# Edges counted in 162 groups of 256 with bands of 12 places, instead of 110 groups of 375 with bands of 16

## The chip, the cores and the metric

The kernel runs on one core of a Trainium2 chip. The metric is the device time of one execution in microseconds, median of the runs. Engines are called as in the profile: PE is TensorE's matmuls and PEld its weight loads, DVE is VectorE, ACT ScalarE, POOL GpSimd, SP SyncE. A row of the profile names a line of the kernel (L521), an engine, an operation and the tiles written and read.

## The reference

Two layers of a graph network over 1250 nodes with 1024 features and 41,250 edges, sorted by destination. The first layer is a relational convolution with two edge types, the second an attention over edges.

```python
h = relu(layernorm(x))
# layer 0: t5 norm, then for r in (0, 1):
    w = (edge_type == r)
    sums = segment_sum(h[src] @ W_rel[r] * w, dst); cnt = segment_sum(w, dst)
    out = x @ W_root + bias + sums / max(cnt, 1)
x = x + h + elu(out) @ wo
# layer 1: h = relu(layernorm(x)) @ W; e = exp(-leaky_relu(al[src] + ar[dst]))
x = x + elu(segment_sum(e * h[dst], src) / (segment_sum(e, src) + 1e-5))
```

## The kernel before

The kernel does not gather rows. It counts how many edges of each type lead from each node to each other node, in a table `cnt` (source within a tile of 128, tile of the source and type, destination), and turns the segment sums into matmuls with that table. The change is in the counting, in `fast_arm`.

**Counting.** The edges, in order of destination, are cut into NG groups of J chunks of PE_ edges, one edge to a partition. For a chunk, DVE builds `key` (L520): for each edge a row of 2 T W columns (T = 10 tiles of sources, two types, W places of destinations), with a one where the column number equals the edge's key. For two groups at a time it builds `lo` (L495, `low_hots`): a one-hot row of 128 for the source within its tile. PE multiplies the two (L521) into the accumulator `acc` of the group, so that `acc` holds the counts for W consecutive destinations, beginning at the first destination of the group. A node whose edges reach over a group's end is finished by a carry: a matmul of 2 T columns (L524) that adds the last chunk's edges of that node to the next group's accumulator. Its one-hot rows `hot_ck` are made by `carry_hots` in four portions. ACT loads the group's first destination into a register (`values_load`, L526) and writes the accumulator into `cnt` at that column (the eviction, L528). Evictions overlap by columns, so each waits for the one before.

**What stands around it.** In the same stage, PE multiplies the normalized rows of ten tiles `t` with the weights of layer 0: 16 products for a tile (L721, `mm<-w,hT`, 429 columns, two passes each). After product `i` of tile `t` as many chunks are emitted as keep the two in step:

```python
want = min(NG * J, -(-NG * J * max(t * SK + i + 1 - late, 0) // (T * SK - 6 - late)))
some(want - done)
```

`plan` puts the other work of the stage at fixed products: the statistics of a later tile (L543), its normalized rows `h` (`norm`, L558), its square sums and their root (`square`, L564 and L566), the two times four transposes of the next tile (`turn`, L576, at products 8 and 10), the copies that scale them into `hT` (`scaled`, L583, at 9 and 12), and the three parts of the previous tile's result `y` (L597 to L614, at 3, 7 and 10). The order written in these loops is the order on PE, DVE and ACT (a manual schedule).

**Banks.** Accumulators with `q % 4 == 3` have a PSUM bank of their own; the others take turns in three banks that they share with the transposes:

```python
def bank(name, dtype=F32):
    return ps.tile([128, 4, 128], dtype, name=name, tag="tp", bufs=3)
...
acc = (own_bank if q % 4 == 3 else bank)("acc").rearrange("p a b -> p (a b)")
```

A bank is free again when ACT has evicted or copied what is in it. `key` has five buffers, `lo` two.

**Afterwards.** The means over neighbours (L798) read `cnt` and `y` tile by tile, then follow the rest of layer 0 and layer 1. If a group's destinations reach over its band, `count_over` sees it, and a general arm computes everything again.

Of the kernel before, what the change touches and what calls it, by code (L numbers as in the profile page):

```python
# [8 lines left out]
F32 = mybir.dt.float32  # L9
# [17 lines left out]
N = 1250  # L27
T = 10
ROWS = [min(128, N - t * 128) for t in range(T)]
PE_ = 125  # L30
J = 3
GE = J * PE_
NG = 110
W = 16
NPAD = 1280


# [373 lines left out]
def fast_arm(tc, ctx, edges, firsts, w_root, conv_bias, wo, w_gat, a_gat, out,  # L411
# [6 lines left out]
    F = w_root.shape[1]  # L418
# [53 lines left out]
    with ExitStack() as c1:  # L472
# [28 lines left out]
        def carry_hots(q, q1):  # L501
            nc.vector.tensor_tensor(hot_ck[:, q:q1], iota_ck[:, None, :].to_broadcast([PE_, q1 - q, 2 * T]),
                                    ck[:, q:q1, None].to_broadcast([PE_, q1 - q, 2 * T]), ALU.is_equal)

        def chunks():

            for q in range(NG):
                if q % 2 == 0 and q // 2 not in los:
                    low_hots(q)
                if q in (10, 40, 75):  # L510
                    carry_hots(q, {10: 40, 40: 75, 75: NG}[q])
                acc = (own_bank if q % 4 == 3 else bank)("acc").rearrange("p a b -> p (a b)")
                a3 = acc[:, :2 * T * W].rearrange("p (c w) -> p c w", w=W)
                if q:

                    last = los[(q - 1) // 2][:, :, ((q - 1) % 2) * J + J - 1]
                    carry = (a3[:, :, 0:1], last, hot_ck[:, q - 1, :, None])
                for j in range(J):
                    key = hot.tile([PE_, 2 * T * W], BF16, name="key")
                    nc.vector.tensor_scalar(key, iota_key, keys[:, q, j:j + 1], None, op0=ALU.is_equal)  # L520
                    nc.tensor.matmul(acc[:, :2 * T * W], los[q // 2][:, :, (q % 2) * J + j], key, start=(j == 0),  # L521
                                     stop=(j == J - 1))
                    if q and j == 0:
                        nc.tensor.matmul(*carry, start=False, stop=False)  # L524
                    if j == J - 1:
                        b = nc.values_load(first[0:1, q:q + 1], engines=[mybir.EngineType.Activation],  # L526
                                           min_val=0, max_val=N - 1)
                        nc.scalar.activation(cnt_w[:, :, bass.ds(b, W)], a3, AF.Copy)  # L528
                    yield
# [86 lines left out]

        tile_of = room[1][:PE_, :NG * J].bitcast(I32).rearrange("p (q j) -> p q j", j=J)
        block, d = (room[1][:PE_, i * NG * J:(i + 1) * NG * J].rearrange("p (q j) -> p q j", j=J) for i in (1, 2))
        step, firstf, limit, over = (room[2][:PE_, a * NG:b * NG] for a, b in ((1, 2), (2, 3), (3, 6), (6, 9)))
        limit, over = (v.rearrange("p (q j) -> p q j", j=J) for v in (limit, over))  # L620

        for i in range(2):
# [13 lines left out]
        def carried():  # L636


            nc.vector.tensor_tensor(step[:, :NG - 1], first[:, 1:], first[:, :NG - 1], ALU.subtract)
            nc.vector.tensor_scalar(step[:, NG - 1:], first[:, NG - 1:], -1.0, float(N), op0=ALU.mult, op1=ALU.add)  # L640

            for j in range(J):
                nc.gpsimd.tensor_scalar(limit[:, :, j], step, -1.0 if j < J - 1 else 0.0, W - 1.0,
                                        op0=ALU.add, op1=ALU.min)
            nc.gpsimd.tensor_copy(firstf, first)
            nc.vector.tensor_tensor(ck, d[:, :, J - 1], step, ALU.is_equal)
            nc.vector.scalar_tensor_tensor(ck, block[:, :, J - 1], 1.0, ck, op0=ALU.add, op1=ALU.mult)
            carry_hots(0, 10)

        worst = small("worst")  # L650

# [20 lines left out]
        def clear_if_odd():  # L672

            odd = nc.values_load(n_odd, engines=[mybir.EngineType.Activation], min_val=0, max_val=8192)
            with tc.If(odd > 0):
# [23 lines left out]
        late_plan = {(1, 1): lambda: square(1), (1, 2): lambda: norm(2), (1, 12): lambda: square(2),  # L699
                     (2, 1): lambda: count_over(), (2, 4): lambda: turn_worst(), (2, 6): lambda: worst_over(),  # L700
                     (2, 12): lambda: clear_if_odd()}
        done, late = 0, 5
        SK = 2 * KD
        for t in range(T):
            pys[t] = ps.tile([128, 2, 512], F32, name="mm")
            for i in range(SK):
# [18 lines left out]
                done = max(done, want)  # L725
# [689 lines left out]
@with_exitstack  # L1415
def gnn_kernel(
    ctx: ExitStack,
    tc: tile.TileContext,
    x: bass.AP,
    src: bass.AP,  # L1420
    dst: bass.AP,
    etype: bass.AP,
    ln_w: bass.AP,
    w_rel: bass.AP,
    w_root: bass.AP,
    conv_bias: bass.AP,
    wo: bass.AP,
    w_gat: bass.AP,
    a_gat: bass.AP,
    edges: bass.AP,  # L1430
    firsts: bass.AP,
    w_cat: bass.AP,
    lnw_cols: bass.AP,
    out: bass.AP,
):


    nc = tc.nc
    D = x.shape[1]
    F = w_root.shape[1]  # L1440
    KD = D // 128
    assert x.shape[0] == N and NG * GE == src.shape[0] and F % 2 == 0

    const = ctx.enter_context(tc.tile_pool(name="const", bufs=1))
    big = ctx.enter_context(tc.tile_pool(name="big", bufs=1))

    def large_tiles():
        return ([big.tile([128, D + 2], F32, name=f"x{t}", tag=f"x{t}")[:, :D] for t in range(T)],
                big.tile([128, 2 * T * NPAD], F16, name="cnt", tag="cnt"),
                [big.tile([128, D + 2], F32, name=f"w{k}", tag=f"w{k}") for k in range(KD)])  # L1450


    xs, cnt_raw, wt = large_tiles()
    wcat = [w[:, :3 * F].rearrange("p (r f) -> p r f", r=2) for w in wt]

    def load_x(t):
        nc.sync.dma_start(xs[t][:ROWS[t]], x[t * 128:t * 128 + ROWS[t], :])

    def loads(part):

        if part == 0:
            for c in (slice(0, 512), slice(512, D)):
                nc.sync.dma_start(xs[0][:, c], x[:128, c])
        for k in range(1) if part == 0 else range(1, KD):
            nc.sync.dma_start(wt[k][:, :3 * F], w_cat[k * 128:(k + 1) * 128, :])
            if k == 3:
                load_x(1)
        if part == 0:
            return
        nc.sync.dma_start(bias, _bcast_rows(conv_bias, 128, F))  # L1470
        for t in range(2, T):
            load_x(t)

    eps5 = const.tile([128, 1], F32, name="eps5")
    nc.vector.memset(eps5, 1e-5)
    eps6 = const.tile([128, 1], F32, name="eps6")
    nc.vector.memset(eps6, 1e-6)
    ones = const.tile([128, 1], F32, name="ones")
    lnw = const.tile([128, KD], F32, name="lnw")
    nc.scalar.dma_start(lnw, lnw_cols)  # L1480

    nc.scalar.activation(ones, eps5, AF.Sqrt)
    bias = const.tile([128, F], F32, name="bias")
    ident = const.tile([128, 128], F32, name="ident")
    make_identity(nc, ident)
    n_odd = const.tile([1, 1], I32, name="n_odd")

    meta = const.tile([128, 2376], F32, name="meta")
    parts, at = [], 0
    for size in (NG * J, NG * J // 2, NG * T, 3 * 128, T * W, T, NG, NG):  # L1490
        parts.append(meta[:PE_, at:at + size])
        at += size
    keys = parts[0].rearrange("p (q j) -> p q j", j=J)
    lows = parts[1].bitcast(F16).rearrange("p (q j) -> p q j", j=J)
    hot_ck = parts[2].bitcast(BF16).rearrange("p (q c) -> p q c", c=2 * T)
    iota_lo = parts[3].bitcast(F16).rearrange("p (l j) -> p l j", j=2 * J)
    nc.vector.memset(ones, 1.0)
    iota_key, iota_ck, ck = parts[4].bitcast(F16), parts[5].bitcast(F16), parts[6]
    firsts_at = meta[:, at - NG:at].bitcast(I32)
    nc.gpsimd.iota(iota_key, pattern=[[1, 2 * T * W]], base=0, channel_multiplier=0,  # L1500
                   allow_small_or_imprecise_dtypes=True)
    nc.gpsimd.iota(iota_lo, pattern=[[1, 128], [0, 2 * J]], base=0, channel_multiplier=0,
                   allow_small_or_imprecise_dtypes=True)
    nc.gpsimd.iota(iota_ck, pattern=[[1, 2 * T]], base=1, channel_multiplier=0,
                   allow_small_or_imprecise_dtypes=True)
    nc.gpsimd.memset(cnt_raw.rearrange("p (c n) -> p c n", n=NPAD)[:, :, N:], 0.0)

    with ExitStack() as arm:
        fast_arm(tc, arm, edges, firsts, w_root, conv_bias, wo, w_gat, a_gat, out, ident, eps5, eps6, lnw, const,
                 big, wt, wcat, bias, xs, cnt_raw, meta, keys, lows, hot_ck, ck, firsts_at, n_odd, iota_lo, iota_key, iota_ck,  # L1510
                 loads)

    odd = nc.values_load(n_odd, min_val=0, max_val=8192)
    with tc.If(odd > 0):
        with ExitStack() as arm:
            xs, cnt_raw, wt = large_tiles()
            general_arm(tc, arm, x, src, dst, etype, ln_w, w_rel, w_root, conv_bias, wo, w_gat, a_gat, out,
                        ident, ones, eps5, eps6, const, [w[:, :D] for w in wt], xs, cnt_raw)
# [6 lines left out]
def _laid_out(inputs):  # L1525

    import numpy as _np

    lists = _np.stack([inputs['src'], inputs['edge_type_2'], inputs['dst']])
    rel, root = inputs['L0_gnn_W_rel'], inputs['L0_gnn_W_root']  # L1530
    half = root.shape[1] // 2
    return {
# [32 lines left out]
```

## Time and profile before

| | |
|---|---|
| median of 3 runs | 592.57 us (592.41 to 592.61) |
| profiled execution | 591.38 us |
| span of the profile | 589.6 us |
| products L721 | x320 passes, 143.7 us busy |
| chunks L521 | x330, 72.3 us busy |
| carries L524 | x109, 19.8 us busy |
| keys L520 on DVE | x330, 85.2 us busy |
| low halves L495 on DVE | x55, 30.3 us busy |
| evictions L528 on ACT | x110, 49.9 us busy |

Busy times of overlapping instructions on PE are counted once, and the recorded duration of a matmul reaches to its last write, so what a matmul costs PE is read from the distance of starts, not from its duration.

### The profile page before, as it was taken

What the parts mean: (1) busy time and instruction counts of PE and PEld (TensorE: products, weight loads), DVE (VectorE), ACT (ScalarE), POOL (GpSimd) and SP (SyncE); (2) the same over time, 40 slices, a digit from 0 to 9 for tenths busy, and PEclk for the clock granted to TensorE, in tenths of its full rate; (3) what the DMA queues carried; (4) which work ended last, traced back from release to release, by engine and by line L of the source; (5) the groups of instructions that cost most, each with busy time, mean ns of one, the idle gap of its engine ahead of it and who ended that gap; (6) DMA issues with size and microseconds to landing.
All of it is one profiled execution on the core that took longest, in us unless ns stands there. A gap on an engine that the chain in (4) does not pass through costs nothing.

```text
span 589.6 us, 8473 instructions
## 1 busy us (share of the span) xinstructions
PE 577.0 (98%) x2848; PEld 419.4 (71%) x2848; DVE 417.9 (71%) x1031; ACT 274.3 (47%) x642; POOL 27.9 (5%) x42
## 2 busy tenths in 40 slices
PE   8999999999999999999999999999999999999994
PEld 5666666666665776776766788888888778888873
DVE  5889887898773666648899926141749988887732
ACT  4666566655643000002332124253727488887722
POOL 5010000000000000000000000000033000000000
PEclk9999999999999999999999999999999999999998
DMA  8950111101106910010015730000010122222221
GB/s 287 345 142 6 36 37 37 36 2 36 29 0 214 245 42 36 37 72 37 36 72 164 209 100 1 0 1 1 2 37 2 37 93 88 71 83 82 99 69 51
DMA packets 21931, 43.82 MB, mean 74 GB/s; under 512 B 2638, under 2 KB 7886, under 8 KB 21876
## 3 DMA queue, kind: packets, MB, share of 16 engines
q1 hardware_dynamic: 20308, 38.05, 19.2%
q0 software_dynamic: 1424, 5.12, 4.6%
q8 instruction: 24, 0.39, 0.3%
q14 instruction: 31, 0.25, 0.1%
q10 hardware_dynamic: 144, 0.00, 0.0%
HBM read 24.53 MB, written 13.52 MB: 65 GB/s over the span
## 4 chain that ended last, share of the span: by engine, by line
PE 80%; DVE 11%; issue 3%; DMA 3%; ACT 2%; SPq 0%; POOL 0%; ACTq 0%; DVEq 0%; POOLq 0%
PE mm L721 17%; PE mm L798 12%; PE mm L989 11%; PE tp L1159 11%; PE acc L521 7%; PE mm L1159 7%; PE mm L844 5%; PE z L989 5%; DMA w<-in_w_cat_dram 3%; DVE cnt L1051 2%; DVE hm L1138 2%; PE tp L576 1%; DVE cnt L1049 1%; ACT d L1097 1%; DVE zm L1134 1%
## 5 line engine op out<-in xcount | busy, mean ns | idle before, releaser
L721 PE MATMUL mm<-w,hT 128*128 128x429 f32 (+1 forms) x320 | 143.7, 535 | 0.9 <-DMA w<-in_w_cat_dram 0.9
L520 DVE TENSOR_SCALAR key<-meta 125x320 bf16<-125x320 f16 x330 | 85.2, 300 | 24.1 <-PE acc L521 12.0
L528 ACT ACTIVATE cnt<-acc 128x320 f32 x110 | 49.9, 453 | 69.5 <-PE acc L521 60.9
L521 PEld LDWEIGHTS <-lo 125*128 125x128 bf16 x330 | 40.5, 126 | 50.4 <-issue 37.0
L798 PE MATMUL mm<-y,cnt 128*128 128x286 bf16 (+3 forms) x600 | 75.2, 285 | 0.4 <-DVE y L614 0.4
L521 PE MATMUL acc<-key,lo 125*128 125x320 bf16 x330 | 72.3, 303 | 0.0
L798 PEld LDWEIGHTS <-cnt 128*128 128x128 f16 (+1 forms) x600 | 59.5, 99 | 14.7 <-issue 1.0
L721 PEld LDWEIGHTS mm<-w,hT 128*128 128x128 f32 (+1 forms) x320 | 51.4, 191 | 6.2 <-issue 3.3
L989 PE MATMUL mm<-w,a 128*128 128x257 f32 (+3 forms) x192 | 44.5, 379 | 0.0
L809 ACT ACTIVATE bias<-bias 128x286 f32<-128x286 f32 (+1 forms) x10 | 4.4, 442 | 80.2 <-DVE bias L808 80.2
L989 PEld LDWEIGHTS mm<-w,a 128*128 128x128 f32 (+1 forms) x192 | 35.7, 187 | 5.5 <-ACT h L1015 0.2
L844 PE MATMUL mm<-wo,meta 128*128 128x512 f32 (+1 forms) x80 | 37.6, 592 | 0.0
L1097 ACT ACTIVATE d<-meta,score 128x128 f32<-128x128 f32 x84 | 27.2, 389 | 10.7 <-DVE d L1114 10.7
L1159 PE MATMUL tp<-hm,zm 128*128 128x512 f32 (+1 forms) x120 | 30.1, 400 | 0.5 <-ACT tp L1165 0.5
L495 DVE TENSOR_TENSOR lo<-meta 125x768 bf16<-125x768 f16 x55 | 30.3, 551 | 0.1
L1097 ACT ACTIVATE d<-meta,tenths 128x128 f32<-128x128 f32 x84 | 27.2, 390 | 0.0
L1159 PEld LDWEIGHTS tp<-hm,zm 128*128 128x128 f32 (+1 forms) x120 | 21.6, 184 | 5.9 <-ACT tp L1165 0.6
L1159 PE MATMUL tp<-hh,zh 128*128 128x512 f32 (+3 forms) x60 | 23.8, 396 | 0.0
L1159 PE MATMUL tp<-parts,zl 128*128 128x512 f32 (+3 forms) x60 | 23.7, 395 | 0.0
L1159 PE MATMUL tp<-hh,parts 128*128 128x512 f32 (+1 forms) x60 | 23.7, 395 | 0.0
L1159 PE MATMUL tp<-parts 128*128 128x512 f32 (+1 forms) x60 | 23.6, 393 | 0.0
L844 PEld LDWEIGHTS mm<-wo,meta 128*128 128x128 f32 (+1 forms) x80 | 14.4, 187 | 12.9 <-issue 12.1
(207 smaller groups left out, 1007.1 us busy)
## 6 DMA issues: line engine op xcount, KB each, us to landing
x<-h POOLq DMA_DIRECT2D x9, 512.0 KB, 4.6
xd<-x SPq DMA_DIRECT2D x9, 512.0 KB, 2.6
x<-in_x_dram SPq DMA_DIRECT2D x8, 512.0 KB, 12.1
w<-in_L_gnn_W_dram SPq DMA_DIRECT2D x8, 512.0 KB, 7.1
w<-in_w_cat_dram SPq DMA_DIRECT2D x8, 429.0 KB, 9.9
squares<-cnt SPq DMA_DIRECT2D x10, 320.0 KB, 3.3
d<-squares SPq DMA_DIRECT2D x40, 80.0 KB, 2.2
d<-xd SPq DMA_DIRECT2D x9, 256.0 KB, 2.8
```

Source lines behind the costliest of these rows:

```text
L495: nc.vector.tensor_tensor(los[q // 2], iota_lo, lows[:, q:q + 2, :].rearrange("p q j -> p (q j)")[:, None, :].to_broadcast([PE_, 128, 2 * J]),
L520: nc.vector.tensor_scalar(key, iota_key, keys[:, q, j:j + 1], None, op0=ALU.is_equal)
L521: nc.tensor.matmul(acc[:, :2 * T * W], los[q // 2][:, :, (q % 2) * J + j], key, start=(j == 0), stop=(j == J - 1))
L528: nc.scalar.activation(cnt_w[:, :, bass.ds(b, W)], a3, AF.Copy)
L721: nc.tensor.matmul(pys[t][:ROWS[t], r, :F + HF], hTs[t][0][:, k, :ROWS[t]], wcat[k][:, r, :], start=(k == 0), stop=(k == KD - 1))
L798: nc.tensor.matmul(pm[:n, r, :f], cnt[:k, h, r, t * 128:t * 128 + n], ybs[h][:k, s, r, :f], start=(h == 0 and s == 0), stop=(h == T - 1 an ...
L844: nc.tensor.matmul(po[:n, c, :], oT[:, i, :n], wo_of[i][:, cs], start=(i == 0), stop=False)
L989: nc.tensor.matmul(o[:a.shape[2], :c1 - c0], a[:, k, :], b[k][:, c0:c1], start=(start and k == 0), stop=(k == KH - 1), skip_group_check=no ...
L1051: nc.vector.transpose(turned_tot.rearrange("p (c t j) -> p c t j", c=4, t=T), tot.rearrange("p (t c i) -> p c t i", t=T, c=4))
L1097: nc.scalar.activation(form[:, t - t0, :], rows[:, s, :], AF.Exp, bias=n[:, t:t + 1], scale=scale)
L1138: engine.tensor_tensor(hms[t][:n, :D], low(t)[:n].bitcast(F32), hhs[t][:n, :D].bitcast(F32), ALU.subtract)
L1159: nc.tensor.matmul(sums_of[s, c][:n], at(sets[s % 2][f], t, t + 1)[:k, 0, :n], h[:k, c * HD:c * HD + HD], start=(t == 0 and f == "h"), sto ...
```

## The change

The groups become smaller: two chunks of 128 edges instead of three of 125, 162 groups instead of 110, with a band of 12 destinations instead of 16. A chunk's matmul, key and eviction have 240 columns instead of 320, `lo` is made for two groups at a time as before (512 instead of 768 elements a row). The last group is padded on the host with edges that match no key. The portions of `carry_hots` and the start of the chunks (`late`, one product later) move along.

```diff
-PE_ = 125
-J = 3
+PE_ = 128
+J = 2
 GE = J * PE_
-NG = 110
-W = 16
+NG = 162
+W = 12
...
+        CARRIES = {15: 60, 60: 111, 111: NG}
...
-                if q in (10, 40, 75):
-                    carry_hots(q, {10: 40, 40: 75, 75: NG}[q])
+                if q in CARRIES:
+                    carry_hots(q, CARRIES[q])
...
-            carry_hots(0, 10)
+            carry_hots(0, 15)
...
-        done, late = 0, 5
+        done, late = 0, 6
...
-    meta = const.tile([128, 2376], F32, name="meta")
+    meta = const.tile([128, 2816], F32, name="meta")
...
-    lists = _np.stack([inputs['src'], inputs['edge_type_2'], inputs['dst']])
+    behind = (0, NG * GE - inputs['src'].shape[0])
+    lists = _np.stack([_np.pad(inputs['src'], behind, constant_values=32767), _np.pad(inputs['edge_type_2'], behind),
+                       _np.pad(inputs['dst'], behind, mode='edge')])
```

In the changed kernel the lines of the stage lie two further down: L523 is the chunk, L526 the carry, L528 the register, L530 the eviction, L578 the transposes, L585 the scaled copies, L723 the products.

More of the change, by code (lines that the diff above doesn't have):

```diff
@@ L618, in fast_arm @@
         block, d = (room[1][:PE_, i * NG * J:(i + 1) * NG * J].rearrange("p (q j) -> p q j", j=J) for i in (1, 2))
-        step, firstf, limit, over = (room[2][:PE_, a * NG:b * NG] for a, b in ((1, 2), (2, 3), (3, 6), (6, 9)))
+        step, firstf, limit, over = (room[2][:PE_, a * NG:b * NG] for a, b in ((1, 2), (2, 3), (3, 3 + J), (3 + J, 3 + 2 * J)))
         limit, over = (v.rearrange("p (q j) -> p q j", j=J) for v in (limit, over))
@@ L1441, in gnn_kernel @@
     KD = D // 128
-    assert x.shape[0] == N and NG * GE == src.shape[0] and F % 2 == 0
+    assert x.shape[0] == N and 0 <= NG * GE - src.shape[0] < GE and F % 2 == 0
     const = ctx.enter_context(tc.tile_pool(name="const", bufs=1))
@@ L1486, in gnn_kernel @@
     n_odd = const.tile([1, 1], I32, name="n_odd")
-    meta = const.tile([128, 2376], F32, name="meta")
+    meta = const.tile([128, 2816], F32, name="meta")
     parts, at = [], 0
-    for size in (NG * J, NG * J // 2, NG * T, 3 * 128, T * W, T, NG, NG):
+    for size in (NG * J, NG * J // 2, NG * T, J * 128, T * W, T, NG, NG):
         parts.append(meta[:PE_, at:at + size])
```

## The prediction

> **What bounds the kernel now.** I read the page first: span, busy shares, slices.
>
> ```profile
> span 589.6 us, 8473 instructions
> PE 577.0 (98%) x2848; PEld 419.4 (71%) x2848; DVE 417.9 (71%) x1031; ACT 274.3 (47%) x642; POOL 27.9 (5%) x42
> ...
> PEclk9999999999999999999999999999999999999998
> ```
>
> TensorE is the bound and runs at its full granted clock. The edges are counted in the first 182 us. The table by stretches gives that stage from 24.5 us, where the loads are in, to its last count:
>
> ```profile
> 24.50:181.70 157.20, 157.20 (x757) 97.70 (x756) 130.88 (x444) 95.56 (x232) 8.56 (x18) 1.00 0.20 44
> ```
>
> PE is never idle, DVE is busy for 130.9 of 157.2 us, ACT for 95.6 (61%). The timeline of PE alone gives prices, as differences of starts, since the durations overlap:
>
> ```profile
> 43.03 0.18 PE L524 MATMUL acc<-meta,lo 125*128 125x20 bf16 x1
> 43.06 0.97 PE L721 MATMUL mm<-w,hT 128*128 128x429 f32 x2
> 43.86 0.44 PE L521 MATMUL acc<-key,lo 125*128 125x320 bf16 x2
> 44.14 0.88 PE L721 MATMUL mm<-w,hT 128*128 128x429 f32 x2
> 44.86 0.30 PE L521 MATMUL acc<-key,lo 125*128 125x320 bf16 x1
> 45.00 0.18 PE L524 MATMUL acc<-meta,lo 125*128 125x20 bf16 x1
> 45.02 0.46 PE L521 MATMUL acc<-key,lo 125*128 125x320 bf16 x2
> ```
>
> A chunk of 320 columns holds PE for 0.14 us, a carry for 0.03, a product (two passes) for 0.72, but for 0.80 where a carry stands just ahead of it (43.06 to 43.86): the carry is too short to cover the load of the product's weights. Over the whole stretch the means are 140.6, 26.7, 722 and 803 ns.
>
> ACT looks idle, but its timeline and the rows of its queue say otherwise:
>
> ```profile
> 99.88 0.44 ACT L528 ACTIVATE cnt<-acc 128x320 f32 x1 [0.53 <-PE acc L524]
> 100.60 0.48 ACT L528 ACTIVATE cnt<-acc 128x320 f32 x1 [0.28 <-ACT cnt L528]
> 101.31 0.44 ACT L528 ACTIVATE cnt<-acc 128x320 f32 x1 [0.23 <-ACT cnt L528]
> ```
>
> ```profile
> L526 ACTq TENSOR_LOAD <-meta x110: 272/278/1110, 9.3 to 180.8; - x110
> L526 ACTq FUSED_REGOPS  x110: 147/147/166, 9.9 to 181.2; - x110
> ```
>
> Three evictions that had nothing to wait for follow each other by 0.715 us, though each lasts 0.44. Between them ACT's queue loads the group's first node into a register: 278 ns, then 147, 18 and 42 with the gaps between them. So an eviction costs 0.715 us whatever its width, and ACT's busy share hides it.
>
> The last view is the timeline of PE and ACT at a bank's reuse:
>
> ```profile
> 58.96 1.13 ACT L583 ACTIVATE hT<-tp,lnw 128x128 f32<-128x128 f32 x4
> ...
> 59.89 0.44 PE L521 MATMUL acc<-key,lo 125*128 125x320 bf16 x2
> ```
>
> Accumulators of groups with q%4 below 3 share three banks with the transposes. The second chunk of the lower row (60.03, group 30) takes the bank that ACT's copies of the upper row give back at 60.09: no slack at all (starts precede recorded ends by 0.06). I worked out this slack for every bank: about 0 at groups 18 and 30, 0.2 at 42, 0.3 to 0.5 us once in most other tiles. PE is the bound today, but ACT stands right behind it.
>
> **The change on PE.** Before 18.64 us PE waits for weights in any case (0.2 us idle there), so I count what follows: 318 chunks before, 315 after (the start one product later moves three chunks behind that wait). A chunk falls from 320 to 240 columns, a width that the trace lacks. The bf16 products of L798 move 286 columns in 122.7 ns (60 of them in 7.36 us), 0.43 a column, so 80 columns are worth at most 34.3; from the carry's 26.7 for 20 columns up to that row the slope is 0.36, so at least 28.9. I take 33, near the wide row: 107.6 a chunk. 318 x 0.1406 = 44.7; 315 x 0.1076 = 33.9: -10.8 us (-9.5 to -11.2). Carries after that point go from 106 to 157: +51 x 0.0267 = +1.4. By the order of instructions, a carry stands directly before a product 66 times instead of 42: +24 x 0.081 = +1.9. Four transposes in a row hold PE 109 ns each, which I read as the load of f32 weights; a chunk of 107.6 covers it but for 0 to 6 ns, at 73 places 0 to 0.4 us: I take 0.1. Sum on PE: -7.4 us, between -5.8 and -7.9.
>
> **The other engines.** DVE: a key costs 0.214 us start to start, 330 of them 70.6; 324 narrower ones lie between 52 (in proportion) and 69 (no fall). Low halves, 55 x 0.469 = 25.8, become 81 of two thirds the width, 25 to 38; carry hots +1.1. At its worst DVE rises by 12 to 143 us of some 155, likelier it falls; keys end 1.3 to 1.7 us ahead of their matmul in half of the cases: nothing on the path. POOL's narrower constants end before use: nothing. The first nodes grow by 28 KB in a load phase that moves some 320 GB/s: +0.1 us. Padding needs no chip time. The spread of the lists is safe: worked out from the reference's lists, no group of 256 reaches further than 10 places, so the general arm stays off.
>
> ACT gets 52 more evictions. Narrower ones (0.44 to about 0.36 us) don't help, since the register chain sets 0.715. Per tile of 18.15 us today: 11 x 0.715 = 7.9, plus what other work adds to the distance between two evictions, from the shortest distances in the trace: copy of y 0.46, of its rest 0.49, root and four scaled copies 0.80, four copies 0.60, normalized rows 0.75, square and root 2.0, together 5.1. Sum 13.0. After: 16.2 x 0.715 + 5.1 = 16.7 us, while PE's tile shrinks to 18.15 - 7.4/9 = 17.3. ACT would be loaded to 96%, with four banks to smooth bursts of up to 4 us (copies, square and root together: 3.8 to 4.0 in the trace).
>
> The Trainium skill, Perfetto Trace Analysis, "Optimizing Scalar/DVE Operations", gives about 51 ns of fixed access cost for a ScalarE instruction on PSUM and advises grouping into larger operations once the engine is saturated. By that price alone 52 more evictions are an estimated 2.7 us of ACT, and the sum would keep PE's gain; the 0.715 us of the trace makes them 37 us. The advice speaks against the change, its price understates it.
>
> **Where ACT holds PE up.** I follow one tile in the changed order (the fourth), with the durations above, from the start of the second four transposes as zero. PE: transposes 0.44, four products, seven chunks, three carries (0.44 + 2.89 + 0.75 + 0.08): it wants the transposes' bank back, for the third group on that ring, at 4.15. ACT: the first eviction can start when its last chunk, behind the next product, is done, 1.54; the next, 0.715 on, 2.26; normalized rows, then the third at 3.63; the four scaled copies behind it end at 4.99, and the bank is free 0.06 earlier, 4.93. PE stands for 0.78 us. Today the same stretch (55.41 to 60.03) takes PE 4.62 and ACT 4.68. The second transposes of that tile already waited for the bank of the first: only two groups now lie between them, 0.61. I did the same for all tiles, with the slow register loads that the trace has after each square (0.87, then 0.45 us, while the residual's DMA runs). Waits, by tile from the end of tile 0: 1.6, 2.0, 3.0, 0.9, 1.4, 0, 1.4, 1.7, 0, 0.1: 12.1 us. The same rules on the old order return most of the measured slacks within 0.05 us, and 0.5 us of waits that the trace lacks, so I take 11.6. With all register loads at 278 ns it would be 10.
>
> **Sum.** -7.4 + 11.6 + 0.1 = +4.3 us. The profiled execution is 591.38 (span 589.6 and 1.8 around it); the median of the runs is 592.57, 1.2 above. The rest of the span only shifts. The last eviction, due some 3.7 us before the stage's last product ends (182.5 against 186.1 today), stays hidden. Forecast 592.57 + 4.3 = 596.9 us; its own range, with waits of 9 to 14 and PE's bounds, 593.8 to 600.5.
>
> **Rivals.** A: *ACT keeps up and PE keeps its gain.* It needs banks back some 0.8 us earlier per tile than my count, for instance if the queue hides the register load behind a wait. For it: ACT's 61%. Against: 0.06 us of slack today and evictions 0.715 apart with nothing to wait for. It gives 592.57 - 7.3 = 585.3; the time is below today's as long as the waits stay under 7.3 us. Chance 0.10.
>
> B: *waits just cancel the gain*, 6.1 to 8.5 us of them: 591.4 to 593.8, within 0.2%, about what a measurement of this kernel can tell from no change. Chance 0.07.
>
> C: *ACT becomes the full bound*: other work doesn't overlap the register chain at all, or loads are slow far more often (0.6 to 1.0 us is common up to 26 us). A tile is then 11.6 + 6.6 (the ACT work in it by durations) = 18.2 plus the waits of PE for bursts, some 19: about +8 us, 600 to 603. Chance 0.08.
>
> The granted clock stays at 1.00 even from 7 to 13 us, where PE idles 0.8 us in all, so I add nothing for it. The Trainium skill, TensorE: Matmul & The Clock Gate, "A second HAM failure mode: psum-queue depth-cycling", tells of a clock that falls back when PE idles often between groups; no run here shows that.
>
> D: *the change does something else* (general arm runs): excluded above, under 0.01.
>
> Main case 0.75. The range of 592 to 600.5 leaves out A, a part of B and the end of C. Slower by over 0.2%: 0.83, faster 0.10.
>
> **What the profile after would show.** Right: L523 at some 225 to 270 ns x324, L530 x162 still 0.715 apart at its densest, PE idle 9 to 13 us before L523 and L578 with ACT (scaled copies L585, evictions L530) as releaser, first product of the last tile near 175 instead of 171 us, the stage from 190.2 on unchanged at 399 us. Wrong: no PE idle in the stage, or DVE's key as releaser; evictions less than 0.6 us apart; or a granted clock below 1.

## The result, and the profile after

The changed kernel takes 593.88 us (median of 12 runs, 592.93 to 594.58), the kernel before 592.48 in the same comparison (12 runs). The ratio is 1.0023, with a 95% interval of 1.0015 to 1.0031: slower by 1.4 us, where 4.3 were forecast. The profiled execution took 593.43 us, 2.05 above that of before: 1.0 us of it is in the counting stage, 0.1 between that and the last matmul, 0.9 behind the last matmul. Single executions differ by about as much as that last part, so the sum below goes by medians. Later comparisons put the kernel before at 592.2 to 592.4.

The head of the page after, and the counting stage in the table by stretches (columns: PE, PEld, DVE, ACT, POOL busy with counts, granted clock, DMA share, GB/s):

```profile
span 591.6 us, 8893 instructions
...
PE 571.1 (97%) x2894; PEld 412.1 (70%) x2894; DVE 412.0 (70%) x1051; ACT 284.2 (48%) x694; POOL 25.6 (4%) x41
...
L530 ACT ACTIVATE cnt<-acc 128x240 f32 x162 | 63.5, 392 | 61.0 <-PE acc L523 38.5
...
L523 PE MATMUL acc<-key,lo 128*128 128x240 bf16 x324 | 61.6, 268 | 4.7 <-ACT cnt L530 3.9
```

```profile
24.50:182.70 158.20, 151.89 (x804) 90.83 (x803) 126.39 (x466) 106.23 (x287) 8.18 (x18) 1.00 0.20 45
```

PE, which was busy for all of the stage, now idles for 6.3 us of it by its recorded durations. By the distances of starts, each beyond what the same instructions in the same order usually take, it waits some 8.6 us. The clock is unchanged. DVE is busy for 126.4 of 158.2 us, less than before. The page names the releaser at the chunks, ACT's eviction. One such wait, in the timeline of PE and ACT:

```profile
64.21 1.03 ACT L566 ACTIVATE sq<-h 128x1024 f32<-128x1024 f32 x1
...
65.12 0.27 PE L523 MATMUL acc<-key,lo 128*128 128x240 bf16 x1
65.15 0.19 ACT L566 ACTIVATION_READ_ACCUMULATOR sq<-h 128x1 f32 x1
...
65.37 0.29 ACT L568 ACTIVATE rms<-ssq,eps 128x1 f32<-128x1 f32 x1
66.03 0.44 ACT L530 ACTIVATE cnt<-acc 128x240 f32 x1 [0.37 <-issue]
66.52 0.27 PE L523 MATMUL acc<-key,lo 128*128 128x240 bf16 x1 [1.12 <-ACT cnt L530]
66.62 0.18 PE L526 MATMUL acc<-meta,lo 128*128 128x20 bf16 x1
66.65 0.61 PE L723 MATMUL mm<-w,hT 128*128 128x429 f32 x1
66.75 0.44 ACT L530 ACTIVATE cnt<-acc 128x240 f32 x1 [0.29 <-ACT cnt L530]
```

ACT squares a tile; its queue stands until the square is done, issues the root (65.37), loads the register, and evicts only at 66.03. PE's next group needs that bank and starts 1.40 us after the last chunk (65.12 to 66.52) instead of 0.1. The two evictions at the end are 0.72 us apart: the width of 240 columns changed the median duration of an eviction (377 ns, from 441) and not this spacing. The register rows are those of before:

```profile
L528 ACTq TENSOR_LOAD <-meta x162: 270/276/1188, 9.7 to 182.1; - x162
L528 ACTq FUSED_REGOPS  x162: 147/147/170, 10.2 to 182.4; - x162
```

### The profile page after: what moved, and what is told of

It reads as the page before. It is cut to its first block, busy times and chain, and to the rows that moved or that the text cites. A ratio compares the mean times of both kernels' runs of the same rounds, so it can differ in the third digit from the quotient of the medians.

```text
span 591.6 us, 8893 instructions
## 1 busy us (share of the span) xinstructions
PE 571.1 (97%) x2894; PEld 412.1 (70%) x2894; DVE 412.0 (70%) x1051; ACT 284.2 (48%) x694; POOL 25.6 (4%) x41
## 5 line engine op out<-in xcount | busy, mean ns | idle before, releaser
L723 PE MATMUL mm<-w,hT 128*128 128x429 f32 (+1 forms) x320 | 145.8, 542 | 1.7 <-DMA w<-in_w_cat_dram 1.7
L530 ACT ACTIVATE cnt<-acc 128x240 f32 x162 | 63.5, 392 | 61.0 <-PE acc L523 38.5
L522 DVE TENSOR_SCALAR key<-meta 128x240 bf16<-128x240 f16 x324 | 74.9, 277 | 4.6 <-PE acc L523 1.8
L523 PEld LDWEIGHTS <-lo 128*128 128x128 bf16 x324 | 35.7, 114 | 44.4 <-issue 23.7
L523 PE MATMUL acc<-key,lo 128*128 128x240 bf16 x324 | 61.6, 268 | 4.7 <-ACT cnt L530 3.9
L723 PEld LDWEIGHTS mm<-w,hT 128*128 128x128 f32 (+1 forms) x320 | 48.8, 190 | 6.2 <-issue 3.7
L495 DVE TENSOR_TENSOR lo<-meta 128x512 bf16<-128x512 f16 x81 | 34.1, 421 | 26.0 <-PE acc L526 25.1
L526 PEld LDWEIGHTS <-lo 128*128 128x128 bf16 x161 | 18.3, 114 | 24.1 <-issue 24.0
L526 PE MATMUL acc<-meta,lo 128*128 128x20 bf16 x161 | 29.4, 183 | 0.0
```

The lines of the kernel that those rows point to most:

```text
L495: nc.vector.tensor_tensor(los[q // 2], iota_lo, lows[:, q:q + 2, :].rearrange("p q j -> p (q j)")[:, None, :].to_broadcast([PE_, 128, 2 * J]),
L723: nc.tensor.matmul(pys[t][:ROWS[t], r, :F + HF], hTs[t][0][:, k, :ROWS[t]], wcat[k][:, r, :], start=(k == 0), stop=(k == KD - 1))
```

## The experiments

The theory: PE's own sum falls by about the forecast 7.4 us, and ACT's turn-around (register chain, square with its root, banks) gives 8 to 9 us back. Rivals: smaller groups cost PE itself more than counted (1); DVE feeds PE late (2); register loads slow the stage in general (3); the 162 register chains alone saturate ACT (4).

**No register chain.** In the changed kernel and in the kernel before, the eviction goes to a column known when the program is built:

```diff
-b = nc.values_load(first[0:1, q:q + 1], engines=[mybir.EngineType.Activation], min_val=0, max_val=N - 1)
-nc.scalar.activation(cnt_w[:, :, bass.ds(b, W)], a3, AF.Copy)
+b = q * (N - 1) // (NG - 1)
+nc.scalar.activation(cnt_w[:, :, b:b + W], a3, AF.Copy)
```

> The changed kernel, but each eviction writes to a column fixed when the program is built, so ACT loads no register (the table of counts comes out shifted by some places; the work stays the same). Theory (PE gains 8.0 us in the stage, and 8.75 us of PE's idle time, seen in the trace after, come from ACT, whose evictions follow each other by 0.715 us because of the register chain): the idle time falls under 1 us, the time to 592.5 - 8.0 + 0.3 = 584 to 586 us. Rival 1 (PE itself pays for the smaller groups: weight loads, carries and starts): no more than 1 us off 593.9. Rival 2 (DVE's keys and low halves arrive late): 593 to 594 us.

Measured 586.8 us, ratio 0.9903 (0.9887 to 0.9919): 7.1 under the changed kernel, a little above the range. PE's waits from 21 us on fell from 8.6 to 1.9 us, by distances of starts.

> The kernel before with the same edit: columns fixed when the program is built, no register loads on ACT. Theory: PE never waited for ACT there, so nothing changes: 592.5 us, within 0.7. Rival 3 (register loads slow the stage in general, through the queue or through traffic): a fall of 2 us or more, in which case the static version of the changed kernel says little about the change.

Measured 592.22 us, ratio 0.9998 (0.9989 to 1.0007): nothing. So register loads cost nothing as such in the kernel before; they cost where ACT is what PE waits for. With both runs, rivals 2 and 3 fall. Of the 1.9 us left, 1.5 stand at two places like this one (timeline of PE and ACT, the changed kernel with fixed columns, where L577 are the transposes and L584 the scaled copies):

```profile
89.76 1.14 ACT L584 ACTIVATE hT<-tp,lnw 128x128 f32<-128x128 f32 x4
...
90.95 0.66 PE L577 MATMUL tp<-ident,h 128*128 128x128 f32 x4 [0.58 <-ACT hT L584]
```

The second four transposes of a tile wait for the bank of the first four, which ACT empties until 90.90.

**The root later.** The square's root leaves its place behind the square and is emitted two products later (likewise where the first tiles have plans of their own):

```diff
             13: lambda t: t + 2 < T and square(t + 2),
+            15: lambda t: t + 2 < T and root(t + 2),
```

> The changed kernel with the root of the square sums (ACT, small) emitted two products after the square instead of right behind it, the registers loaded as before. In the trace after, ACT's queue stands until the square has ended before it can issue the root, and only then begins the next register load: 2.1 to 2.75 us from one eviction to the next, once a tile. Theory: freed of that, ACT catches up in each tile; of 8.75 us of PE's idle time 2 to 4 are left, 586 to 589 us. Rival 4 (the 162 register chains alone saturate ACT, wherever the square stands): 592 to 594 us.

Measured 587.31 us, ratio 0.9912 (0.9898 to 0.9926): 6.6 us of the changed kernel's time, with all 162 register chains in place; 2.7 us of waits remain. Rival 4 falls: the chains fit, if ACT's queue doesn't stand behind the square.

> The kernel before with the root emitted two products after the square. Theory: no wait of PE for ACT is there to be taken away, so 592.3 us within 0.7. Rival (a later root helps by something other than ACT's turn-around): 590 us or less.

The same edit in the kernel before: 592.17 us, 0.9998 (0.9989 to 1.0007). There was no wait to take away.

**The band and the groups, apart.** Three chunks of 128 in 108 groups with bands of 14 (`J = 3`, `NG = 108`, `W = 14`, the plans of before; worked out from the reference's lists, no group of 384 reaches further than 13 places), and two chunks of 128 in 162 groups with bands of 16:

> Three chunks of 128 in 108 groups with bands of 14 places: the narrower band without the smaller groups. Theory: chunks fall from 330 of 140.6 ns to 324 of 119 to 121, -7.4 us on PE; evictions (108), carries (107) and the carries ahead of products stay as before the change, and ACT's turn-around of 13.0 us a tile fits into PE's 17.3. Waits 0 to 1.5 us. 585 to 587 us, faster than both kernels. Rival 1 (narrow chunks don't pay on PE): 590 to 592.5 us.

Measured 586.75 us, ratio 0.9909 (0.9895 to 0.9923). The narrower band without smaller groups is worth 5.5 us, with 0.8 us of waits. (It is 14 and not 12 here, and the chunks have 128 edges, so this isn't the change's own band alone.)

> The smaller groups without the narrower band: 162 groups of two chunks of 128 edges, bands of 16 places as before the change. Theory (what the groups cost is 52 more carries and 24 more of them ahead of a product, about +3.3 us on PE, and ACT's 52 more register chains, which make PE wait; the band only pays on PE): 324 chunks of 320 columns save 0.8 us, PE's own sum is +2.5, waits of 4 to 7 us remain though PE's tile is longer: 598.5 to 602 us. Rival 1 (groups cost only PE, no waits): 594.5 to 595.5.

Measured 602.11 us, ratio 1.0162 (1.0148 to 1.0177): the smaller groups alone cost 9.7 us, just above the range; PE waits some 7.4 us in that stage. From there the band of 12 gains 8.2 us (602.11 to 593.88), so the change is a gain that doesn't quite pay for a larger loss.

**The banks.** All accumulators and transposes take turns in one set of four banks:

```diff
-return ps.tile([128, 4, 128], F32, name=name, tag="own", bufs=1)
+return bank(name)
...
-return ps.tile([128, 4, 128], dtype, name=name, tag="tp", bufs=3)
+return ps.tile([128, 4, 128], dtype, name=name, tag="tp", bufs=4)
```

> The changed kernel with all accumulators and transposes in one set of four banks, instead of one bank for every fourth group and three shared. Theory with banks handed out in the order in which they were given back (in program order): the waits of the second transposes for the bank of the first (0.74 us, two or three tiles) go, those on evictions after square and root stay: 590.5 to 592.5 us, that is 1.5 to 3.5 under the changed kernel. Banks handed out strictly in turn, as in the prediction: waits for the scaled copies near products 13 to 14 of most tiles, time falls by 4 us or more.

Measured 591.34 us, ratio 0.9985 (0.9976 to 0.9993): 2.5 under the changed kernel, and the waits of second transposes (0.73 us each at two places of the changed kernel) are gone; those on evictions behind the square stay (1.4 us at 65.0, 1.0 at 101.2). That fits banks that are handed out in the order in which they were given back; the strict order of the prediction would have had 4 us or more.

**Together.**

> Three chunks of 128 in 108 groups with bands of 14 and the later root together. Theory: of the 0.8 us of waits that bands of 14 left, at most 0.8 us go: 585.8 to 586.8 us, the fastest of these kernels or level with the one without the later root. Rival: the two gains (5.5 and 6.6 us) add: 580 us.

Measured 586.20 us, ratio 0.9898 (0.9884 to 0.9913). The gains don't add: three chunks leave next to nothing (0.8 us) for the later root to take away.

> The changed kernel (162 groups of two chunks, bands of 12, registers loaded) with both the later root and the one set of four banks. Theory: 2.7 us of waits were left with the later root alone, 1.5 of them in two tiles where the second transposes wait for the bank of the first; those go: 585.5 to 586.8 us, level with three chunks and bands of 14. Rival 4 (162 register chains saturate ACT): 587.3 us or more, as with the later root alone.

Measured 585.36 us, ratio 0.9882 (0.9865 to 0.9898), a little under the range and faster than both kernels: 162 groups with bands of 12, the later root and the four shared banks. ACT's timeline shows what the later root does:

```profile
95.37 1.10 ACT L566 ACTIVATE sq<-h 128x1024 f32<-128x1024 f32 x1
96.32 0.24 ACT L566 ACTIVATION_READ_ACCUMULATOR sq<-h 128x1 f32 x1
96.41 0.82 ACT L530 ACTIVATE cnt<-acc 128x240 f32 x2
97.12 0.28 ACT L572 ACTIVATE rms<-ssq,eps 128x1 f32<-128x1 f32 x1
```

Two evictions follow the square at once (96.41): the register of the first was loaded ahead of the square, that of the second while it ran. PE's stage in this kernel (table by stretches) is almost without gaps:

```profile
24.50:179.00 154.50, 153.96 (x815) 92.41 (x815) 125.99 (x467) 104.24 (x286) 8.39 (x18) 1.00 0.23 52
```

> The changed kernel with columns fixed when the program is built and the one set of four banks: no register chain and no wait for a bank by the order of the transposes (the counts come out shifted). Theory: this is what PE's own sum gives, the two waits of 0.74 us that the static columns left are gone: 585 to 586 us. Rival 1 (PE pays more for smaller groups than counted): 586.8 us, no change from the static columns alone.

Measured 585.09 us, ratio 0.9877 (0.9861 to 0.9894): with neither register chain nor that wait, next to nothing more is to be had than the kernel above has. 592.4 - 585.1 = 7.3 us is the worth of the change on PE, since fixed columns alone were worth nothing in the kernel before. Rival 1 falls.

## Why the prediction was right or wrong

**Right: PE's own sum, with some luck.** -7.4 forecast, -7.3 measured, but its parts were off in ways that cancel. From start to start a chunk takes 102 to 103 ns, and 108 to 109 directly behind a carry: 104.8 in the mean, not 107.6, that is 0.9 us less over 315 chunks. The fall from 140.6 is 36 ns, more than the 34.3 that the prediction called the most. The run with bands of 16 splits it: a chunk of 320 columns takes 137.8 ns in the mean there, so the 80 columns are worth 33.0, as forecast, and 2.8 came with the other chunks (128 edges instead of 125, two to a group), which the prediction had at nothing. On the other side, a product's first pass behind a chunk takes 369 ns instead of 364 (medians, 63 of them, 0.3 us, where I had 0.1 for weight loads). In the first tile PE idles for a weight 0.65 us instead of 0.22 (0.80 in the run with fixed columns and shared banks), and that last run still has some 0.3 us of waits.

**Right in part: where the loss comes from.** ACT's evictions stand 0.715 us apart whatever their width, and banks come back late. Taking away the chain (7.1 us) or the square's hold (6.6) gave back nearly what the theory said, and one set of banks 2.5. But by starts 4.7 of the 8.6 us are waits for evictions behind a square, where the tile that the prediction works out has them at the banks of the scaled copies. DVE was nothing on the path, as argued, and the rest of the kernel only shifted. By the price of the Trainium skill (Perfetto Trace Analysis, "Optimizing Scalar/DVE Operations"), some 51 ns of access for an instruction, the prediction estimated 2.7 us of ACT for 52 more evictions, which would have kept PE's gain. The 0.715 us of this case decides; the runs show the gain as soon as ACT is off the path.

**Wrong: the size of the waits.** The step that failed is the term of 11.6 us of waits in the sum; it was 8.8 (593.88 - 585.09). In *Where ACT holds PE up* I had the three shared banks taken strictly in turn, so that the third group after the second transposes wanted their bank. The timeline of PE and ACT after shows that it doesn't:

```profile
112.69 0.60 PE L578 MATMUL tp<-ident,h 128*128 128x128 f32 x4
...
113.85 0.27 PE L523 MATMUL acc<-key,lo 128*128 128x240 bf16 x1
...
113.98 0.38 PE L523 MATMUL acc<-key,lo 128*128 128x240 bf16 x2
...
114.35 0.37 ACT L530 ACTIVATE cnt<-acc 128x240 f32 x1 [0.52 <-PE acc L523]
...
115.02 0.37 PE L523 MATMUL acc<-key,lo 128*128 128x240 bf16 x2
...
116.03 1.13 ACT L585 ACTIVATE hT<-tp,lnw 128x128 f32<-128x128 f32 x4
```

The second transposes start at 112.69. Behind them the groups 92, 93 and 94 begin on the shared banks: at 113.85, with the second chunk of the row of 113.98 (114.09), and with the second chunk of the row of 115.02 (115.13). By the strict order group 94 should have waited for copies that end at 117.16; it didn't wait at all. The trace fits banks that are handed out in the order in which the program gives them back: group 92 was evicted from 114.35 on, ahead of the copies, and its bank is taken first; the transposes' bank comes later.

The kernel before could have told this. Followed through the program, the two rules name different banks there too, in three places, and two of them are groups 18 and 30, to which the prediction gave no slack. Its own rows have group 30's chunk start at 60.03, 0.06 us before the copies' end at 60.09. Where PE does wait for ACT, it starts 0.05 us after the end (90.90 and 90.95, 66.47 and 66.52 in the rows above). So that chunk had not waited for the copies: by the rule that fits, its bank was that of group 28. The 0.06 us that the prediction put down to recorded ends was the sign that its rule was wrong.

With the rule that fits, the waits come where the trace after has them: at the second transposes of two tiles (0.73 us each) and on evictions behind the square (five waits of 0.6 to 1.3 us in four tiles). By recorded durations, from 21 us on (PE's waits with us in total, times, longest):

```profile
PE acc L523 <- ACT cnt L530: 3.9, 5, 1.1
...
PE tp L578 <- ACT hT L585: 1.2, 2, 0.6
...
PE acc L523 <- ACT hT L585: 0.8, 1, 0.8
```

The waits of chunks for copies, which the prediction had in nearly every tile, are absent but for one near 25 us (0.9 by starts), in a tile that has a plan of its own.

A recount of the waits by this rule, an estimate of mine whose working is not shown here, gives some 6 us. That is 2.6 short of the 8.6 in the trace, so the strict rule was wrong by more than the miss shows, and something else was counted too small. At one of the largest of these a slow register load (0.86 us at 62.62 us) comes one eviction earlier than I had placed it. Whether such loads explain all of the rest was not tested and stays open.

**The rivals.** A (ACT keeps up, 585.3) did not come about in the changed kernel; with the later root and shared banks it does, at 585.36. B (waits just cancel the gain) was the nearest in time: 8.8 us of waits lie beyond its 8.5. C did not come about: the later root shows that the chains fit. The upper end of the prediction's own range is 600.9 by its terms, not 600.5, which matters to nothing here.

## What to carry to other kernels

An engine's busy share (61% for ACT here) does not show its turn-around: read the shortest distance between two instructions of the kind that a change multiplies, and the queue's rows between them. Where a bound engine shares buffers with such an engine, test the rule by which the pool hands out buffers on the trace of before, at each place where two rules differ: a start before the end of the supposed releaser refutes the rule, however small the difference. And a small instruction that waits for a long one ahead of it can hold everything queued behind it: moving the root two products later was worth 6.6 us here, 0 where nobody waited.

## What was not expected of the hardware

A register load takes 0.27 us, but 0.86 to 1.2 at one place or two in nearly every tile, while the residual's accumulating DMA runs (issued at 61.02, some 5 us to landing, slow load at 62.62 us); that the DMA is the cause was not tested. Where an eviction is narrower but its queue's work is the same, the spacing of evictions that follow each other does not move at all (0.714 us at 320 and at 240 columns). And a chunk directly behind a carry takes longer from start to start than any other, whatever comes next: 108 to 109 ns against 102 to 103 at 240 columns, 142 against 136 at 320 in the run with bands of 16, and 155 against 138 in the kernel before (medians). Why stays open.
